# Moving transposes between TensorE and DRAM in a four-layer graph network

## The chip, the cores and the metric

The kernel runs on one core of a Trainium2 chip. The metric is device time in microseconds from launch to end, the median of several runs. The profile is of one further execution; its span goes from the first to the last instruction. All data are 32-bit floats.

## The reference

There are 64 graphs of 256 nodes with 256 features each, `x`, and a weighted adjacency, `adj`. Four graph layers follow one another; around each of them stands a residual sum and a layer norm, `x = layernorm(x + layer(x, adj))`.

```python
# layer 0: 4 heads of 64, sigmoid attention, normalised by degree
X, q, k = heads(lrelu(x @ W_lin + b_lin)), heads(lrelu(x @ W_q)), heads(lrelu(x @ W_k))
adj_h = adj[:, None] * sigmoid(einsum('bhxd,bhyd->bhxy', q, k) * scale)
dis = deg ** -0.5                       # deg: sum of adj_h over its last axis
Y = einsum('bhxy,bhyd->bhxd', dis[..., :, None] * adj_h * dis[..., None, :], X)
# then a layer norm of its own
# layer 1: 8 heads of 32, masked softmax attention
q, k, v = heads(x @ Wq + bq), heads(x @ Wk + bk), heads(x @ Wv + bv)
scores = where(adj > 0, q k^T / sqrt(32), NEG)
out = softmax(scores) v, heads joined, @ Wo + bo
# layer 2: (adj @ x + eps * x) @ W1 (256 to 1024), rms norm, silu, @ W2 (1024 to 256)
# layer 3: one head; e depends on a row term and a column term
Wh = x @ W;  e = leaky_relu(Wh.a1 [:, None] + Wh.a2 [None, :], 0.2)
h = softmax(where(adj > 0, e, NEG)) @ Wh
out = gelu(layernorm(h))
```

## The kernel before

**Tiles.** One graph is the unit of work: `graph(...)` (line 238) is called for `b` from 0 to 63 and lists the operations of all four layers. A 256x256 matrix lies in SBUF as 128 partitions by 512 words, its two row halves side by side; `two(v)` (line 166) gives it as 128 x 2 x 256.

**A planner sets the order.** No operation is issued where it is listed. `op(engine, cost, fn, writes, reads, turn=...)` records it, and `Plan.order` (line 94) then lays out all graphs at once: it keeps a clock for each engine, takes at each step the operation that can start first (ties by due time, graph and index), and gives each tile a slot in a pool when its first operation is taken. `SLOTS` (line 33) is the number of slots: 42 of 512 words (`s`), 10 of 1024 (`d`), 8 PSUM banks (`p`), 8 DRAM buffers (`h`). The order on each engine is therefore fixed before the program runs, and each engine works through its own list in order; waits between engines are by semaphore. SP issues all DMAs, through one queue, also in order.

**Turns.** ACT needs another table for Sigmoid, Exp, Silu and Gelu. Operations with these functions, and the products that feed them, carry a turn, `4 * min(b + ROUND[layer], graphs - 1 + TAIL[layer]) + function` (line 250), and a turn is worked off before the next begins. `ROUND = 0, 2, 5, 7` says how many rounds after its first layer a graph does each later one; so in the middle of the run four groups of graphs are at work in four layers in the same round. `TAIL = 0, 2, 3, 5` caps the round for the last graphs, which then share their turns.

**Transposes.** Attention weights are made with rows in the partitions, and the product that follows wants them the other way. There are two ways. `transposed` (line 266, with `transpose`, line 258) does four 128x128 transposes on TensorE into a PSUM bank; `copy` (line 297) has ACT bring that to SBUF. `far_transposed` (line 271) does 32x32 blocks with one DVE instruction into `eb` (line 275), and then lets DMAs put the blocks in place by way of a DRAM buffer `far`. With `in_order` (lines 278 to 288) these are four writes of 64 KB in pieces of 512 bytes (line 281) and four reads of 64 KB in pieces of 128 bytes (line 285). Without it, one write of 256 KB (line 289) and four reads of 64 KB (line 291), and the columns come out in another order, which the reader's pattern undoes.

Where they are used before the change:

- layer 0's output, `yb = far_transposed(ps, "yT", in_order=False)` (line 478), read by two DVE multiplications by `dis` (line 482);
- layer 1's input `xT` by TensorE (line 492); layer 1's exponentials by a far path of their own, for two heads at a time: a DVE transpose of 128x1024 (line 521), one 512 KB write (line 523) and four 128 KB reads (line 525); the product with `v1` is line 536;
- layer 3's input, `xT3 = far_transposed(x, "xT3")` (line 628), read by the product with `w3` (line 637);
- layer 3's exponentials by TensorE and ACT, `eT = copy(transposed(e), "eT")` (line 656), read by `token_major` (line 319).

**Around them.** `softmax` (line 390) masks, scales and takes the minimum on DVE (line 395) and exponentiates with a sum on ACT (line 400). Layer 1's queries get their bias from one DVE addition of 128x512 out of PSUM (line 496); the scores (line 510) need it. Layer 2 has the largest products, line 579 (to 1024 features; ACT brings them in with a bias, line 584) and line 622 (back to 256). After the layer-3 product come statistics (line 333), a power on GpSimd (line 346), an affine step (lines 383 and 386), Gelu (line 661), the residual (line 662), a last norm and the store (line 664).

Of the kernel before, what the change touches and what calls it, by code (L numbers as in the profile page):

```python
# [10 lines left out]
AF = mybir.ActivationFunctionType  # L11
OP = mybir.AluOpType

P = 128
# [5 lines left out]
PE_MM, PE_TR = 432, 109  # L20
# [6 lines left out]

WORDS = {"s": 516, "d": 1024, "b": 2048, "c": 32, "p": 512, "h": 1024}
AHEAD = 14

ROUND = 0, 2, 5, 7
TAIL = 0, 2, 3, 5
SLOTS = {"s": 42, "d": 10, "b": 3, "c": 72, "p": 8, "h": 8}


# [39 lines left out]
class Plan:  # L75
# [9 lines left out]
    def op(self, engine, cost, fn, w=(), r=(), turn=None, mode="full", after=None, size=0):  # L85
        pair = lambda x: x if isinstance(x, tuple) else (x, None)
        w, r = [pair(x) for x in w], [pair(x) for x in r]
        op = Op(engine, cost, fn, w, r, self.graph, turn, mode, after, size)
        op.table = turn is not None and engine == "ACT"
        if op.table:  # L90
            self.turns[turn] = self.turns.get(turn, 0) + 1
        self.ops.append(op)
# [73 lines left out]
def two(v):  # L166

    return v.t.rearrange("p (n c) -> p n c", n=2)
# [69 lines left out]
def graph(plan, nc, c, t, out, b):  # L238

    op = plan.op  # L240
    pe, dve, act, pool = nc and nc.tensor, nc and nc.vector, nc and nc.scalar, nc and nc.gpsimd
    NB = DB = 2
    N = D = 256
# [5 lines left out]
    def turn(layer, func):  # L249
        return 4 * min(b + ROUND[layer], plan.graphs - 1 + TAIL[layer]) + func  # L250

# [6 lines left out]
    def transpose(dst, src, w, r):  # L258

        def fn():  # L260
            for j in range(2):
                for i in range(2):
                    pe.transpose(dst()[:, j, i * P:(i + 1) * P], src()[:, i, j * P:(j + 1) * P], c.ident)  # L263
        op("PE", 4 * PE_TR, fn, [w], [r], mode="transpose")

    def transposed(src):
        ps = Value("p", "ps", 2)
        transpose(lambda: two(ps), lambda: two(src), ps, src)
        return ps

    def far_transposed(src, name, in_order=True):


        eb, far, dst = Value("s", "eb"), Value("h", "far", 4), Value("s", name, 4)
        op("DVE", 635, lambda: dve.transpose(
            eb.t.rearrange("p (b g i) -> p g b i", b=4, i=32),
            src.t.rearrange("p (n k w) -> p k n w", n=2, k=2)), [eb], [src])
        if in_order:
            F = lambda a: far.t[:64].rearrange("(a z) (y w) -> a (z y) w", a=4, w=P)[a]
            for a in range(4):  # L280
                op("SP", 420, lambda a=a: nc.sync.dma_start(
                    F(a).rearrange("(b j) w -> j b w", b=4),
                    eb.t[32 * a:32 * a + 32].rearrange("j (b w) -> j b w", b=4)), [(far, a)], [eb], after=3000, size=64)
            for a in range(4):
                op("SP", 420, lambda a=a: nc.sync.dma_start(
                    dst.t.rearrange("q (g a i) -> a q g i", g=4, a=4)[a],
                    F(a).rearrange("q (g i) -> q g i", g=4)), [(dst, a)], [(far, a)], after=4500, size=200)
            return dst
        op("SP", 420, lambda: nc.sync.dma_start(far.t[:, :512], eb.t), [(far, i) for i in range(4)], [eb], after=3000, size=256)
        for q in range(4):  # L290
            op("SP", 420, lambda q=q: nc.sync.dma_start(
                dst.t[32 * q:32 * q + 32].rearrange("j (a g) -> j a g", a=4),
                far.t[:, :512].rearrange("(a j) (b g) -> b j a g", a=4, b=4)[q]), [(dst, q)],
                [(far, i) for i in range(4)], after=4200, size=64)
        return dst

    def copy(ps, name):
        dst = Value("s", name, 2)
        op("ACT", 466, lambda: act.copy(dst.t, ps.t), [dst], [ps])  # L299
        return dst  # L300
# [109 lines left out]
    xT, adjT, x, adj = load("x0T", "xT"), load("adjT", "adjT"), load("x", "x"), load("adj", "adj")  # L410
    qk = []
    for w, name in ((c.w0_q, "qT0"), (c.w0_k, "kT0")):
        ps = feature_major(w, xT)
        y = Value("s", name)
# [3 lines left out]
    ps = token_major(xT, lambda: c.w0_l.t, [c.w0_l])  # L418
    v = Value("s", "v0")
# [20 lines left out]
    ps = Value("p", "ps")  # L440
# [18 lines left out]
    dp, dis = Value("c", "dp"), Value("c", "dis")  # L459
# [5 lines left out]
    by_head = lambda ap: ap.rearrange("p (g d) -> p g d", d=HD0)  # L465
    dis_b = lambda: dis.t[:, :8, None].to_broadcast([P, NB * H0, HD0])
    op("DVE", 603, lambda: dve.tensor_tensor(by_head(v.t), by_head(v.t), dis_b(), OP.mult), [v], [v, dis])
    ps = Value("p", "ps", 2)
# [6 lines left out]
                    pe.matmul(two(ps)[i * HD0:(i + 1) * HD0, hp, :], two(v)[:, m, h * HD0:(h + 1) * HD0],  # L475
                              A(h)[:, m, :], start=(m == 0), stop=(m == NB - 1))
    op("PE", 4 * PE_MM, fn, [ps], [v, att], mode="columns")
    yb = far_transposed(ps, "yT", in_order=False)
    y = Value("s", "y", 2)
    for i in range(2):  # L480
        by = lambda ap, i=i: ap.rearrange("p g (i k w) -> p g i k w", i=2, k=2)[:, :, i]
        op("DVE", 345, lambda y=y, i=i, by=by: dve.tensor_tensor(
            by(y.t.rearrange("p (g d) -> p g d", g=4)), yb.t.rearrange("p (i k g w) -> p i g k w", i=2, k=2, g=4)[:, i],
            dis.t[:, :8].rearrange("p (g i) -> p i g", i=2)[:, i, :, None, None].to_broadcast([P, 4, 2, 32]), OP.mult),
            [y], [yb, dis])
    mv, m = stats(y)
    affine(y, mv, m, c.g0, lambda n, xb=xb: two(xb)[:, n, :], [xb])
    x = normed(y, "x1")
# [3 lines left out]
    xT = copy(transposed(x), "xT")  # L492
    xb = plus_row(x, c.c1)
    ps = feature_major(c.w1_q, xT)
    qT1 = Value("s", "qT1")
    op("DVE", 602, lambda ps=ps: dve.tensor_tensor(two(qT1), two(ps), c.b1_q.t[:, :, None].to_broadcast([P, 2, N]), OP.add),
       [qT1], [ps, c.b1_q])

    kT1 = copy(feature_major(c.w1_k, xT), "kT1")
    v1 = copy(token_major(xT, lambda: c.w1_v.t, [c.w1_v]), "v1")  # L500
    av, r = Value("p", "av", 2), Value("c", "r")
    eTs = []
    for hq in range(H1 // 4):
        pss = [Value("p", "ps", 2) for _ in range(4)]

        def fn(hq=hq, pss=pss):
            for n in range(NB):
                for i in range(4):
                    s = slice(i * HD1, (i + 1) * HD1)
                    pe.matmul(two(pss[i])[:, n, :], two(qT1)[s, hq, n * P:(n + 1) * P], two(kT1)[s, hq, :],  # L510
                              start=True, stop=True)
        op("PE", 2 * PE_MM, fn, pss, [qT1, kT1], turn=turn(1, EXP), mode="rows")
        for pair in range(2):


            e, eb, far, eT = Value("d", "e", 4), Value("d", "eb"), Value("h", "far"), Value("d", "eT", 4)
            for i in range(2):
                softmax(pss[2 * pair + i], negmask, HD1 ** -0.5, e,
                        lambda n, i=i, e=e: e.t[:, 256 * (2 * i + n):256 * (2 * i + n + 1)],
                        lambda n, i=i: 2 * i + n, r, lambda n, h=4 * hq + 2 * pair + i: 2 * h + n, turn(1, EXP))  # L520
            op("DVE", 1155, lambda e=e, eb=eb: dve.transpose(eb.t.rearrange("p (b g i) -> p g b i", b=4, i=32),  # L521
                                                             e.t.rearrange("p (g b i) -> p g b i", b=4, i=32)), [eb], [e])
            op("SP", 420, lambda eb=eb, far=far: nc.sync.dma_start(far.t, eb.t), [far], [eb], after=3500, size=512)
            for q in range(4):
                op("SP", 420, lambda far=far, eT=eT, q=q: nc.sync.dma_start(
                    eT.t[32 * q:32 * q + 32].rearrange("j (a g) -> j a g", a=4),
                    far.t.rearrange("(a j) (b g) -> b j a g", a=4, b=4)[q]), [(eT, q)], [far], after=4000, size=128)
            eTs.append(eT)


    def fn():
        for hq in range(H1 // 4):
            for m in range(NB):
                for i in range(4):
                    h = 4 * hq + i
                    pe.matmul(two(av)[i * HD1:(i + 1) * HD1, hq, :], two(v1)[:, m, h * HD1:(h + 1) * HD1],  # L536
                              eTs[h // 2].t.rearrange("p (a h n k i) -> p h k n a i", a=4, h=2, n=2, k=2)[:, i % 2, m],
                              start=(m == 0), stop=(m == NB - 1))
    op("PE", 4 * PE_MM, fn, [av], [v1, *eTs], mode="columns")

    op("DVE", 180, lambda: dve.reciprocal(r.t[:, :16], r.t[:, :16]), [r], [r])
    ps = Value("p", "ps")
    op("PE", PE_TR, lambda ps=ps: pe.transpose(ps.t[:16, :P], r.t[:, :16], c.ident), [ps], [r], mode="transpose")
    rT, far, rb = Value("s", "rT"), Value("h", "far"), Value("s", "rb", H1)
# [7 lines left out]
    yT = Value("s", "yT")  # L552
# [72 lines left out]
    x = normed(plus(ps, xb), "x3")  # L625


    xT3 = far_transposed(x, "xT3")
    v3 = Value("s", "v3", 2)
    V3 = lambda: v3.full.rearrange("p (n c) -> p n c", n=2)  # L630
    s1 = lambda n: V3()[:, n, D:D + 1]
# [21 lines left out]
    r3 = Value("c", "r3")  # L653
    softmax(e, negmask, 1.0, e, lambda n: two(e)[:, n, :], lambda n: n, r3, lambda n: n, turn(3, EXP))
    op("DVE", 70, lambda: dve.reciprocal(r3.t[:, :NB], r3.t[:, :NB]), [r3], [r3])
    eT = copy(transposed(e), "eT")
    ps = token_major(eT, lambda: V3()[:, :, :D], [v3])
    y3 = Value("s", "y", 2)
    mv, m = stats(ps, r3)
# [91 lines left out]
```

## Time and profile before

| | |
|---|---|
| median of 3 runs | 2822.43 us (2820.94 to 2826.75) |
| the profiled execution, its own time | 2825.22 us |
| its span | 2823.4 us |
| instructions | 55149 |
| granted TensorE clock, mean | 0.991 |
| DMA queue of the kernel | 558320 packets, 475.87 MB, 59.2% of 16 engines' span |
| load of an ACT table | 1.283 us, 254 times |

In the profile PE is a TensorE matmul or transpose and PEld the load of its stationary operand, DVE is VectorE, ACT ScalarE, POOL GpSimd, and SPq the queue of DMA issues. A group of instructions is named by its line in the kernel, what it writes and reads, and its shapes; then follow its count, the time in which it was busy (overlaps counted once) and the mean duration of one. Then comes the idle time of the engine just before such instructions, with what ended it. In the chain of work that ended last, each piece begins when what released it was done, so that its pieces don't overlap and add up to the span. A DMA's time to landing is from its issue to its completion.

### The profile page before, as it was taken

How to read it: one execution, taken by the hardware profiler on the slowest of the kernel's cores; microseconds unless marked ns; L12 is line 12 of the kernel's file. 1: busy time of each engine (PE TensorE's matmuls, PEld its weight loads, DVE VectorE, ACT ScalarE, POOL GpSimd, SP SyncE). 2: the span in 40 equal slices, each digit the busy share in tenths (PEclk: the TensorE clock that was granted, in tenths of full speed). 3: DMA queues.
4: the chain of work that ended last, by engine and by line, in shares of the span. 5: the costliest groups of instructions: out<-in, count | busy, mean ns of one | idle time of the engine just before them, and what ended most of it. 6: DMA issues, size and time to landing. Idle time of an engine off the chain costs nothing.

```text
span 2823.4 us, 55149 instructions
## 1 busy us (share of the span) xinstructions
PE 2752.3 (97%) x17092; PEld 2189.6 (78%) x17092; DVE 2494.3 (88%) x7757; ACT 2131.5 (75%) x5054; POOL 585.8 (21%) x902
## 2 busy tenths in 40 slices
PE   8899999999999999999999999999999999999996
PEld 6667777887787878788878878778787778777784
DVE  5788898989899998998899989899989989899975
ACT  3767787778688777877777777878768877686774
POOL 1011211212222222212212212222212221212111
PEclk9999999999999999999999999999999999999998
DMA  4857476646466646665576556556556647475641
GB/s 142 252 151 196 152 202 180 187 134 192 127 193 199 197 135 200 192 179 148 155 192 180 172 163 183 171 167 187 174 149 183 198 141 201 125 194 153 181 123 41
DMA packets 558613, 479.40 MB, mean 170 GB/s; under 512 B 184304, under 2 KB 516976, under 8 KB 558320
## 3 DMA queue, kind: packets, MB, share of 16 engines
q1 hardware_dynamic: 558320, 475.87, 59.2%
q8 instruction: 137, 2.24, 0.4%
q14 instruction: 156, 1.28, 0.2%
HBM read 290.60 MB, written 185.07 MB: 168 GB/s over the span
## 4 chain that ended last, share of the span: by engine, by line
PE 87%; DVE 5%; ACT 3%; DMA 2%; SPq 1%; issue 1%; POOL 0%; DVEq 0%; POOLq 0%; ACTq 0%
PE ps L622 15%; PE ps L308 15%; PE ps L319 14%; PE ps L579 14%; PE ps L510 4%; PE ps L432 4%; PE ps L567 4%; PE ps L637 4%; PE ps L475 3%; PE av L536 3%; PE ps L263 2%; ACT e L400 1%; PE ps L449 1%; DVE e L395 1%; DVE st L333 1%
## 5 line engine op out<-in xcount | busy, mean ns | idle before, releaser
L400 ACT ACTIVATE e<-e,low 128x256 f32<-128x256 f32 x1152 | 575.7, 501 | 73.5 <-DVE low L395 69.8
L622 PE MATMUL ps<-w,hT 128*128 128x256 f32 x2048 | 480.6, 382 | 4.2 <-ACT hT L613 4.2
L579 PE MATMUL ps<-aggT,w 128*128 128x256 f32 x2048 | 470.8, 382 | 2.8 <-ACT aggT L299 1.4
L345 POOL TENSOR_SCALAR mv<-mv 128x2 f32<-128x2 f32 x384 | 123.0, 320 | 1624.8 <-DVE mv L335 1074.0
L579 PEld LDWEIGHTS ps<-aggT,w 128*128 128x128 f32 x2048 | 382.4, 190 | 69.2 <-issue 8.6
L622 PEld LDWEIGHTS ps<-w,hT 128*128 128x128 f32 x2048 | 381.3, 190 | 67.6 <-issue 10.5
L395 DVE CUSTOM_DVE_ANT_0 e<-ps,adj 128x256 f32<-128x256 f32 x1024 | 361.7, 420 | 33.5 <-PE ps L510 32.5
L521 DVE STREAM_TRANSPOSE eb<-e 128x1024 f32<-128x1024 f32 x256 | 310.5, 1225 | 4.7 <-ACT e L400 4.0
L346 POOL TENSOR_TENSOR mv<-mv,mhalf 128x2 f32<-128x2 f32 x384 | 307.7, 801 | 32.0
L584 ACT ACTIVATE hT<-ps,b 128x256 f32<-128x256 f32 x512 | 225.8, 473 | 97.0 <-PE ps L579 66.6
L360 ACT ACTIVATE x<-y,mv 128x256 f32<-128x256 f32 x384 | 216.2, 599 | 61.3 <-DVE mv L356 53.2
L333 DVE BATCH_NORM_STATS2 st<-y 128x6 f32<-128x256 f32 x640 | 242.3, 412 | 1.4
L400 ACT ACTIVATION_READ_ACCUMULATOR e<-e,low 128x1 f32 x1152 | 220.8, 192 | 0.0
L609 DVE SCALAR_TENSOR_TENSOR hT<-hT,r,pr 128x256 f32<-128x256 f32 x512 | 207.3, 474 | 7.0 <-PE pr L606 6.6
L590 DVE TENSOR_TENSOR sq<-sq 128x512 f32<-128x512 f32 x192 | 130.5, 680 | 48.1 <-ACT sq L587 47.0
L438 DVE TENSOR_TENSOR att<-att,adjT 128x512 f32<-128x512 f32 x256 | 165.7, 678 | 5.6 <-ACT att L436 5.5
L587 ACT ACTIVATE sq<-hT 128x512 f32<-128x512 f32 x256 | 163.1, 637 | 2.0 <-DMA far<-eb 0.6
L510 PE MATMUL ps<-kT,qT 32*128 32x256 f32 x2048 | 152.0, 404 | 1.0 <-ACT kT L299 1.0
L462 POOL TENSOR_TENSOR dp<-dp,mhalf 128x8 f32<-128x8 f32 x64 | 109.2, 1707 | 202.7 <-DVE dp L461 175.4
L436 ACT ACTIVATE att<-ps 128x512 f32<-128x512 f32 x256 | 132.3, 603 | 25.0 <-PE ps L622 18.6
L613 ACT ACTIVATE hT<-hT 128x1024 f32<-128x1024 f32 x128 | 129.8, 1051 | 19.5 <-DVE hT L609 17.0
L308 PE MATMUL ps<-x0T,w_q 128*128 128x256 f32 x512 | 132.1, 392 | 7.2 <-DMA x0T<-in_xT 7.2
(108 smaller groups left out, 5526.7 us busy)
## 6 DMA issues: line engine op xcount, KB each, us to landing
far<-eb SPq DMA_DIRECT2D x256, 512.0 KB, 3.5
eT<-far SPq DMA_DIRECT2D x1024, 128.0 KB, 3.9
adj<-in_adj SPq DMA_DIRECT2D x128, 256.0 KB, 4.7
x0T<-in_xT SPq DMA_DIRECT2D x64, 256.0 KB, 3.5
adjT<-in_adjT SPq DMA_DIRECT2D x64, 256.0 KB, 4.4
x<-in_x SPq DMA_DIRECT2D x64, 256.0 KB, 4.8
adj<-in_adjT SPq DMA_DIRECT2D x64, 256.0 KB, 5.3
far<-eb SPq DMA_DIRECT2D x64, 256.0 KB, 2.7
```

Source lines behind the costliest of these rows:

```text
L308: pe.matmul(two(ps)[:, o, :], w.t[:, k, o * P:(o + 1) * P], two(xT)[:, k, :], start=(k == 0), stop=(k == DB - 1))
L319: pe.matmul(two(ps)[:, n, :], two(xT)[:, k, n * P:(n + 1) * P], w()[:, k, :], start=(k == 0), stop=(k == DB - 1))
L333: op("DVE", 328, lambda n=n: dve.bn_stats(st.t[:, 6 * n:6 * n + 6], two(src)[:, n, :]), [(st, n)], [(src, n)])
L346: pool.tensor_tensor(m()[:, :, 2], m()[:, :, 2], c.mhalf[:, :NB], OP.pow)
L360: op("ACT", 492, lambda n=n: act.activation(two(dst)[:, n, :], two(src)[:, n, :], AF.Identity, bias=m()[:, n, 0:1], scale=m()[:, n, 2:3]), ...
L395: op("DVE", 345, lambda n=n: dve.tensor_tensor_reduce(out=E(n), in0=two(logits)[:, n, :], in1=two(negmask)[:, n, :], scale=-scale, scalar= ...
L400: op("ACT", 491, lambda n=n: act.activation(E(n), E(n), AF.Exp, bias=low.t[:, n:n + 1], scale=-1.0, accum_out=r.t[:, col(n):col(n) + 1]), ...
L510: pe.matmul(two(pss[i])[:, n, :], two(qT1)[s, hq, n * P:(n + 1) * P], two(kT1)[s, hq, :], start=True, stop=True)
L521: op("DVE", 1155, lambda e=e, eb=eb: dve.transpose(eb.t.rearrange("p (b g i) -> p g b i", b=4, i=32), e.t.rearrange("p (g b i) -> p g b i" ...
L579: pe.matmul(two(ps)[:, i, :], c.w2_1.t[:, k, (j + i) * P:(j + i + 1) * P], two(aggT)[:, k, :], start=(k == 0), stop=(k == DB - 1))
L584: op("ACT", 357, lambda ps=ps, i=i, j=j: act.activation(Hb(j + i)[:, 0], two(ps)[:, i, :], AF.Identity, bias=c.b2_1.t[:, j + i:j + i + 1]) ...
L622: pe.matmul(two(ps)[:, n, :], Hb(j)[:, 0, n * P:(n + 1) * P], c.w2_2.t[:, j, :], start=(j == 0), stop=(j == HB - 1))
```

## The change

Three numbers `NEAR = 1, 1, 3` say for how many graphs another way is taken than for the rest.

- Layer 0's output: graph 0 is transposed by TensorE and copied by ACT, and one DVE multiplication instead of two follows. All other graphs keep the DRAM way.
- Layer 1's exponentials: graph 0 by TensorE, 8 transposes and two ACT copies for each pair of heads. All others keep the DRAM way.
- Layer 3's input: graphs 61, 62 and 63 by TensorE and an ACT copy, the others through DRAM as before.
- Layer 3's exponentials: graphs 0 to 60 through DRAM, by `far_transposed` with its default `in_order`; graphs 61 to 63 by TensorE and ACT as before.
- Layer 1's query bias, all graphs: two ACT activations of 128x256 out of PSUM with the bias, one for each half, instead of one DVE addition.
- `TAIL` goes from 0, 2, 3, 5 to 0, 2, 3, 4: the last graphs' layer 3 is capped one round earlier.

```diff
+NEAR = 1, 1, 3
-TAIL = 0, 2, 3, 5
+TAIL = 0, 2, 3, 4
...
-    yb = far_transposed(ps, "yT", in_order=False)
     y = Value("s", "y", 2)
-    for i in range(2):
...
+    if b < NEAR[0]:
+        ps = transposed(copy(ps, "yT"))
+        op("DVE", 602, lambda ps=ps, y=y: dve.tensor_tensor(by_head(y.t), by_head(ps.t), dis_b(), OP.mult), [y], [ps, dis])
+    else:
+        yb = far_transposed(ps, "yT", in_order=False)
+        for i in range(2):
...
-    qT1 = Value("s", "qT1")
-    op("DVE", 602, lambda ps=ps: dve.tensor_tensor(two(qT1), two(ps), c.b1_q.t[:, :, None].to_broadcast([P, 2, N]), OP.add),
-       [qT1], [ps, c.b1_q])
+    qT1 = Value("s", "qT1", 2)
+    for o in range(2):
+        op("ACT", 357, lambda ps=ps, o=o: act.activation(
+            two(qT1)[:, o, :], two(ps)[:, o, :], AF.Identity, bias=c.b1_q.t[:, o:o + 1]), [(qT1, o)], [(ps, o), c.b1_q])
...
+            if b < NEAR[1]:
+                eT = Value("d", "eT", 2)
+                for i in range(2):
+                    half = lambda v, i=i: v.t[:, 512 * i:512 * (i + 1)].rearrange("p (n c) -> p n c", n=2)
+                    ps = Value("p", "ps", 2)
+                    transpose(lambda ps=ps: two(ps), lambda e=e, half=half: half(e), ps, e)
+                    op("ACT", 466, lambda ps=ps, eT=eT, half=half: act.copy(half(eT), two(ps)), [(eT, i)], [ps])
+                eTs.append((eT, lambda i, m, eT=eT: eT.t.rearrange("p (h m c) -> p h m c", h=2, m=2)[:, i, m]))
+                continue
...
-    xT3 = far_transposed(x, "xT3")
+    xT3 = copy(transposed(x), "xT3") if b >= plan.graphs - NEAR[2] else far_transposed(x, "xT3")
...
-    eT = copy(transposed(e), "eT")
+    eT = copy(transposed(e), "eT") if b >= plan.graphs - NEAR[2] else far_transposed(e, "eT3")
```

More of the change, by code (lines that the diff above doesn't have):

```diff
@@ L477, in graph @@
     op("PE", 4 * PE_MM, fn, [ps], [v, att], mode="columns")
-    yb = far_transposed(ps, "yT", in_order=False)
     y = Value("s", "y", 2)
-    for i in range(2):
[L481 to L485, printed above, removed]
+    if b < NEAR[0]:
[4 more added lines that the diff above has]
+        for i in range(2):
+            by = lambda ap, i=i: ap.rearrange("p g (i k w) -> p g i k w", i=2, k=2)[:, :, i]
+            op("DVE", 345, lambda y=y, i=i, by=by: dve.tensor_tensor(
+                by(y.t.rearrange("p (g d) -> p g d", g=4)), yb.t.rearrange("p (i k g w) -> p i g k w", i=2, k=2, g=4)[:, i],
+                dis.t[:, :8].rearrange("p (g i) -> p i g", i=2)[:, i, :, None, None].to_broadcast([P, 4, 2, 32]), OP.mult),
+                [y], [yb, dis])
     mv, m = stats(y)
@@ L513, in graph @@
         for pair in range(2):
-            e, eb, far, eT = Value("d", "e", 4), Value("d", "eb"), Value("h", "far"), Value("d", "eT", 4)
+            e = Value("d", "e", 4)
             for i in range(2):
@@ L520, in graph @@
                         lambda n, i=i: 2 * i + n, r, lambda n, h=4 * hq + 2 * pair + i: 2 * h + n, turn(1, EXP))
+            if b < NEAR[1]:
[7 more added lines that the diff above has]
+                continue
+            eb, far, eT = Value("d", "eb"), Value("h", "far"), Value("d", "eT", 4)
             op("DVE", 1155, lambda e=e, eb=eb: dve.transpose(eb.t.rearrange("p (b g i) -> p g b i", b=4, i=32),
@@ L527, in graph @@
                     far.t.rearrange("(a j) (b g) -> b j a g", a=4, b=4)[q]), [(eT, q)], [far], after=4000, size=128)
-            eTs.append(eT)
+            eTs.append((eT, lambda i, m, eT=eT: eT.t.rearrange("p (a h n k i) -> p h k n a i", a=4, h=2, n=2, k=2)[:, i, m]))
     def fn():
@@ L536, in fn @@
                     pe.matmul(two(av)[i * HD1:(i + 1) * HD1, hq, :], two(v1)[:, m, h * HD1:(h + 1) * HD1],
-                              eTs[h // 2].t.rearrange("p (a h n k i) -> p h k n a i", a=4, h=2, n=2, k=2)[:, i % 2, m],
+                              eTs[h // 2][1](i % 2, m),
                               start=(m == 0), stop=(m == NB - 1))
-    op("PE", 4 * PE_MM, fn, [av], [v1, *eTs], mode="columns")
+    op("PE", 4 * PE_MM, fn, [av], [v1, *(eT for eT, _ in eTs)], mode="columns")
     op("DVE", 180, lambda: dve.reciprocal(r.t[:, :16], r.t[:, :16]), [r], [r])
```

## The prediction

> **What bounds the kernel now.** I read the busy line first, then the engines by stage.
>
> ```profile
> PE 2752.3 (97%) x17092; PEld 2189.6 (78%) x17092; DVE 2494.3 (88%) x7757; ACT 2131.5 (75%) x5054; POOL 585.8 (21%) x902
> ```
>
> By stage, the columns are the stretch, its length, and then PE, PEld, DVE, ACT and POOL busy with their instructions, the clock, the DMA share and GB/s:
>
> ```profile
> 70.00:140.00 70.00, 60.71 (x359) 43.53 (x359) 56.88 (x165) 51.51 (x144) 5.25 (x6) 0.90 0.86 253
> ...
> 400.00:800.00 400.00, 398.69 (x2520) 318.67 (x2517) 358.05 (x1127) 310.67 (x743) 79.41 (x125) 1.00 0.60 168
> 800.00:1200.00 400.00, 398.07 (x2524) 317.50 (x2524) 373.89 (x1165) 317.45 (x750) 92.91 (x140) 1.00 0.64 183
> ...
> 2750.00:2824.00 74.00, 45.49 (x190) 36.44 (x188) 38.60 (x129) 33.62 (x68) 13.24 (x25) 0.82 0.17 40
> ```
>
> There are three regimes. In the middle TensorE is idle 1.3 to 1.9 us in 400, so time there is TensorE work, with DVE next at up to 93%. Between 400 and 2500 us all waits of PE that the profile lists come to 5.0 us; the longest group is this (total, times, longest):
>
> ```profile
> PE ps L308 <- ACT xT L299: 1.2, 2, 0.8
> ```
>
> At the start PE idles (400 minus its busy time, stage by stage) 29 us, 7.2 of them before the first load lands; at the end 28.5 us of the last 74. Those two stages are chains of latency, not throughput.
>
> Then the groups of instructions that the edits touch:
>
> ```profile
> L263 PE MATMUL ps<-ident,e 128*128 128x128 f32 x256 | 39.7, 277 | 2.3 <-ACT e L400 2.3
> ...
> L275 DVE STREAM_TRANSPOSE eb<-x 128x512 f32<-128x512 f32 x64 | 44.8, 701 | 5.8 <-ACT x L360 5.8
> ...
> L496 DVE TENSOR_TENSOR qT<-ps,b_q 128x512 f32<-128x512 f32 x64 | 43.5, 679 | 19.0 <-PE ps L308 18.4
> ...
> L584 ACT ACTIVATE hT<-ps,b 128x256 f32<-128x256 f32 x512 | 225.8, 473 | 97.0 <-PE ps L579 66.6 <-PE ps L622 29.9
> ...
> L299 ACT COPY eT<-ps 128x512 f32<-128x512 f32 x64 | 37.5, 586 | 26.6 <-PE ps L263 24.3 <-DMA out<-o 1.9 <-ACT v L299 0.2
> ```
>
> A transpose is said to last 277 ns and its group to be busy 39.7 us (155 ns each), but neighbours overlap. What it takes from the stream is read in the chain that ended last, whose pieces do not overlap:
>
> ```profile
> 1250.30 3.65 PE ps L579 x16
> 1253.95 0.44 PE ps L263 x4
> 1254.38 0.11 PE ps L543
> ```
>
> Four transposes hold the stream 0.44 us, 0.11 each; the same view has 0.87 for eight.
>
> **What the Trainium skill says.** (1) "Perfetto Trace Analysis", Identifying the Most-Contended Engine: matmul busy share is a poor measure, since pipelined PE instructions overlap. This trace agrees: 70.9 us by the mean (256 x 277 ns), 39.7 by the union, 28.2 (64 x 0.44) by the chain. I price with the last. (2) "VectorE: DVE Perf Modes", The three transpose paths: TensorE transposes a full 128x128 into PSUM, the DVE only 32x32 blocks, into SBUF. So the new path needs DMAs to put the blocks in place; the kernel before does just that for the layer-3 input. (3) "DMA: Bandwidth & Descriptors", Anatomy of one DMA: about 2 us of a DMA are fixed, mostly the completion. The same-sized transfers here land 1.8 and 2.6 us after issue, in agreement:
>
> ```profile
> far<-eb SPq DMA_DIRECT2D x256, 64.0 KB, 1.8
> xT<-far SPq DMA_DIRECT2D x256, 64.0 KB, 2.6
> ```
>
> (4) "ScalarE: Activation LUTs", What ACT_TABLE_LOAD costs: 1283 ns and a drain of 1380. The trace shows 1283; in the last stretch the next activation follows with no such drain, so I use 1.28 us.
>
> **The change, part by part.** Sums stand against the profiled execution: 2825.22 us, span 2823.4, so 1.8 us outside; it is 2.8 above the median 2822.43, and I take 2.8 off at the end.
>
> *Layer 3's transposes of e, 61 graphs (0 to 60).* Removed: 61 x 4 TensorE transposes, 61 x 0.44 = 26.8 us from a stream that is full: on the path. ACT loses 61 copies of 586 ns (35.7 us, off the path); one of eight PSUM banks is held less. Added: 61 DVE block transposes of 701 ns (42.8 us) and 61 x 8 DMAs on SP. Bytes are 61 x 0.52 MB = 32 MB, 6.7% of the queue's 475.9; packets are 512 of 512 B and 2048 of 128 B a graph, 156,000, 28% of the queue's 558,320. So its 59.2% share grows by 4 points (by bytes) to 17 (by packets); the 128-B ones are the cheap kind per packet, so I take 7, to about 66%, which leaves room. SP gets 4 issues of 432 and 4 of 621 ns (medians of the same two lines), 4.2 us a graph. The longer way from e to its product (0.70, then issue and 1.8, then issue and 2.6: some 8 to 10 us against 1.6 now) is covered: in the built order the two exponentials of layer 3 stand among the first three of nearly every turn on ACT, ahead of the 16 of layer 1, so between them and the Gelu that needs the result lie some 16 x (501+192) ns = 11 us plus the Silu pair. With that cover gone ACT, PE and DVE would stall behind a late Gelu.
>
> *Queries' bias.* DVE loses 64 x 679 ns = 43.5 us, ACT gains 128 x 473 = 60.5 (L584 is the same operation and shape). Net with the part above and with what graphs 0 and 61 to 63 drop (about 8 us): DVE -9 us, ACT near +30 of 2131. Neither bounds. In front of the scores the wait now stands in ACT's queue; queued behind it there are L584 and the exponentials, but ACT has 25% free and each half starts when its half of the product is ready. Zero; if ACT were late, up to 0.3 us a graph.
>
> *Graph 0 by TensorE in layers 0 and 1.* 4 + 32 transposes, +4.0 us of PE at 0.11. What they save is a trip. In the chain, graph 0's yT leaves the DVE at 37.70 and its use starts at 48.89: 11 us against about 2 by PE and an ACT copy. For the last pair of its layer-1 exponentials the chain shows
>
> ```profile
> 83.70 4.95 DMA far<-eb
> 88.67 5.00 DMA eT<-far
> ```
>
> and the product L536 starts at 104.0; the PE way ends near 82. It also takes 4.2 MB out of 70 to 140 us, where DMA is 86% busy. Of PE's 22 us idle in the first 400 (beyond the first load) I take 7 back; bounds 0 (graph 1 still goes through DRAM and sets the ramp) and 14.
>
> *Last three graphs' layer-3 input by TensorE; last turn one earlier.* Before, in the timeline of the last graph:
>
> ```profile
> 2784.91 1.09 ACT L360 ACTIVATE x<-y,mv 128x256 f32<-128x256 f32 x2 [3.15 <-DVE mv L356]
> ...
> 2786.03 0.71 DVE L275 STREAM_TRANSPOSE eb<-x 128x512 f32<-128x512 f32 x1 [0.61 <-ACT x L360]
> ...
> 2788.64 2.54 SPq L285 DMA_DIRECT2D xT<-far  x4
> ...
> 2796.55 3.65 PE L637 MATMUL ps<-w,xT 128*128 128x258 f32 x8
> ```
>
> From x to its product 10.5 us; by PE 0.44 and a copy of 0.59, with hand-overs 1.2: -9.3. The built order has two table loads fewer (252 for 254); one on the path: -1.3. Against that, four graphs instead of three now share the last Gelu turn: after the last product, before, 15.5 us remain (2807.88 to 2823.4); the new DVE order has 15.3 us of work there, by my count at the page's durations, plus a pow and the store: +2.5. Sum -8; bounds -14 and -2 (graphs 62 and 63 in each other's way). The 12 extra transposes (1.3 us) fall where PE idles.
>
> *Order of the rest.* The planner reorders everything. Counted in the two built orders, PE changes between full, row, column and transpose shapes 1049 times before and 1051 after: no gain or loss. New waits in the middle: 0 to 8 us (PE now waits 0.10 us a graph); I take 2.5.
>
> Sum: -26.8 + 4.0 - 7 - 8 + 2.5 = -35.3; 2825.2 - 35.3 = 2789.9, less 2.8: **2787**.
>
> **Rivals.** *The waits come back* (0.08). DVE, at 93% in places, or the later eT3, makes PE wait 0.4 us a graph: 61 x 0.4 = 24 us, and the ends give little (-4 in all, with the +4.0 paid): 2822 - 27 + 24 - 0 = 2819. For: DVE is close behind. Against: its work per graph is unchanged and PE's 5.0 us of waits show that the order absorbs it.
>
> *SP's queue, slower* (0.05). SP issues in order; eight DMAs a graph, half of them waiting for the other half to land (1.8 us), stand before layer 1's transfers. Up to 4.2 + 1.8 = 6 us of delay meet L536, whose slack the trace does not show. It turns slower when PE loses over (35.3+5.6)/61 = 0.67 us a graph; at 1.0 it is 2787 + 61 = 2848. Against: no PE wait on eT<-far stands in the list for the middle, and SP is issuing about half the time.
>
> *Both ends shrink fully* (0.07): -26.8 + 4 - 18 - 14 = -55: 2768.
>
> *The change doesn't do what it says:* the built PE order has 196 transposes fewer (244 out, 48 in), so that is excluded.
>
> **Chances.** Forecast 0.80. Its own range: -26.8+4-14-14 = -51 to -26.8+4-0-2+8 = -17, so 2771 to 2806. A measurement here can tell about 0.2%, 5.6 us, from no change. Faster: 0.80 + 0.07 + half of the first rival = 0.91; same 0.04; slower 0.05. The range 2771 to 2806 leaves out some 2 in 10.
>
> **What would show it.** PE instructions 16896, group L263's e at 12, PE's busy time 20 to 24 us less. In the middle PE idle still under 3 us in 400; if more, the wait list names DVE (first rival) or DMA eT (second). DMA share near 66%. L536's first start near 80 instead of 104. The last 74 us with some 8 less idle. I am wrong if PE's waits in the middle pass 15 us or the last stretch is no shorter.

## The result, and the profile after

The changed kernel takes 2799.0 us (four runs, 2796.7 to 2804.5) against 2822.1 us before, a ratio of 0.9918 with a 95% interval of 0.9899 to 0.9937: 23 us less. The forecast was 2787, with a range of 2771 to 2806. The profiled execution after is the fastest of its four, 2796.7 us with a span of 2794.9 us; the one before was 2825.22 and 2823.4. The spans differ by 28.5 us.

Engines first, from the page of the changed kernel:

```profile
PE 2728.7 (98%) x16896; PEld 2159.8 (77%) x16896; DVE 2477.0 (89%) x7745; ACT 2150.8 (77%) x5131; POOL 590.6 (21%) x902
```

TensorE has 196 instructions and 23.6 us of busy time less, as expected, DVE 17 us less, ACT 19 more. By stage (columns as before: stretch, length, then PE, PEld, DVE, ACT, POOL, the clock, the DMA share, GB/s):

```profile
70.00:140.00 70.00, 65.41 (x423) 49.23 (x423) 57.78 (x169) 52.16 (x136) 8.85 (x11) 0.92 0.61 183
...
400.00:800.00 400.00, 399.56 (x2496) 317.07 (x2495) 371.41 (x1170) 323.60 (x777) 91.66 (x137) 1.00 0.70 191
800.00:1200.00 400.00, 396.29 (x2476) 313.47 (x2474) 360.09 (x1125) 312.56 (x745) 79.73 (x126) 1.00 0.66 184
...
2000.00:2400.00 400.00, 390.00 (x2407) 307.69 (x2407) 355.32 (x1118) 308.91 (x756) 84.41 (x125) 0.99 0.66 180
...
2720.00:2795.00 75.00, 54.30 (x263) 45.12 (x260) 48.38 (x162) 37.33 (x77) 15.66 (x30) 0.91 0.13 33
```

The start and the end are shorter: PE idles 4.6 us instead of 9.3 between 70 and 140, where the DMA share fell from 0.86 to 0.61, and 20.7 us of the last 75 instead of 28.5 of the last 74. The middle is worse: between 400 and 2400 us PE was never idle for 2 us in a stretch of 400, and now it is for 3.7 and for 10.0. PE's waits between 400 and 2500 us, longest first (total, times, longest):

```profile
PE ps L516 <- ACT kT L300: 6.9, 3, 5.9
PE ps L653 <- DVE hT L625: 2.9, 2, 2.7
PE ps L638 <- ACT hT L600: 1.5, 2, 1.2
PE ps L613 <- DVE sq L608: 1.5, 1, 1.5
```

The queue's share rose to about what was forecast (66%). The small pieces are indeed cheap one by one: over the trace before, a packet of 128 bytes took 13.5 ns of a DMA engine on average, one of 1 KB 59.3 ns.

```profile
q1 hardware_dynamic: 710624, 501.59, 65.1%
```

At the end, the last graph's layer-3 input now takes this way in the timeline:

```profile
2765.32 0.60 ACT L361 ACTIVATE x<-y,mv 128x256 f32<-128x256 f32 x1
...
2768.37 2.01 PE L653 MATMUL ps<-w,xT 128*128 128x258 f32 x8 [0.97 <-ACT xT L300]
```

From the start of x to its product it is 3.05 us instead of 11.64.

The difference of the two spans, put together from PE's busy and idle time (idle is the length of a stretch less PE's busy time in it):

| | forecast | measured | before to after |
|---|---|---|---|
| PE busy (-26.8 + 4.0 + 1.3) | -21.5 | -23.6 | 2752.3 to 2728.7 |
| idle in the first 400 us | -7 | -12.5 | 29.1 to 16.6 |
| idle, 400 to 2600 us | +2.5 | +12.8 | 10.7 to 23.5 |
| idle, 2600 us to the end | -9.3 | -5.2 | 31.4 to 26.2 |
| sum | -35.3 | -28.5 | of 28.5 |

(-9.3 is the forecast's -8 with its 1.3 us of transposes hidden in idle time.) The term that failed is the third: the new waits in the middle.

### The profile page after: what moved, and what is told of

It is laid out like the page before. It is cut to its first block, busy times and chain, and to the rows that moved or that the text cites. A ratio compares the mean times of both kernels' runs of the same rounds, so it can differ in the third digit from the quotient of the medians.

```text
span 2794.9 us, 55587 instructions
## 1 busy us (share of the span) xinstructions
PE 2728.7 (98%) x16896; PEld 2159.8 (77%) x16896; DVE 2477.0 (89%) x7745; ACT 2150.8 (77%) x5131; POOL 590.6 (21%) x902
## 4 chain that ended last, share of the span: by engine, by line
PE 81%; DVE 7%; ACT 5%; DMA 3%; SPq 2%; issue 1%; POOL 0%; DVEq 0%; POOLq 0%; ACTq 0%
PE ps L309 15%; PE ps L320 14%; PE ps L638 13%; PE ps L595 13%; PE ps L516 4%; PE ps L433 4%; PE ps L476 4%; PE av L552 4%; PE ps L583 4%; PE ps L653 3%; ACT e L401 2%; DMA eT<-far 1%; PE ps L450 1%; PE ps L264 1%; DVE st L334 1%
## 5 line engine op out<-in xcount | busy, mean ns | idle before, releaser
L595 PE MATMUL ps<-aggT,w 128*128 128x256 f32 x2048 | 476.7, 384 | 5.3 <-DVE low L396 3.1
L346 POOL TENSOR_SCALAR mv<-mv 128x2 f32<-128x2 f32 x384 | 129.8, 338 | 1610.2 <-DVE mv L336 1056.1
L625 DVE SCALAR_TENSOR_TENSOR hT<-hT,r,pr 128x256 f32<-128x256 f32 x512 | 207.2, 473 | 17.8 <-PE pr L622 17.8
L437 ACT ACTIVATE att<-ps 128x512 f32<-128x512 f32 x256 | 132.2, 602 | 27.8 <-PE ps L638 25.1
```

What stands on the lines that cost most here:

```text
L595: pe.matmul(two(ps)[:, i, :], c.w2_1.t[:, k, (j + i) * P:(j + i + 1) * P], two(aggT)[:, k, :], start=(k == 0), stop=(k == DB - 1))
```

## The experiments

Each of the twelve other kernels is measured beside the kernel before on the same chip; since three chips were used, kernels of different experiments are best compared by their ratios (0.001 is 2.8 us). The table has PE's busy time and idle time by stage from each profile; "far" is the DRAM way of layer 3's exponentials, "bias" the queries' bias on ACT, "ends" the rest of the change. A profile is one execution, up to 6 us from its kernel's median, so differences of 2 or 3 us in these columns say little.

| kernel | what it is | median us | ratio, 95% interval | PE busy | idle, first 400 | 400 to 2600 | last 75 (ends rounded to 1 us) | clock |
|---|---|---|---|---|---|---|---|---|
| before | | 2822.1 to 2825.5 | 1 | 2752.3 | 29.1 | 10.7 | 27.5 | 0.991 |
| order_before | another order | 2820.2 | 0.9980 (0.9972-0.9988) | 2749.5 | 29.0 | 9.6 | 28.4 | 0.992 |
| bias_only | bias | 2821.8 | 0.9986 (0.9980-0.9993) | 2749.9 | 27.1 | 12.4 | 27.7 | 0.992 |
| ends_only | ends | 2803.7 | 0.9927 (0.9915-0.9940) | 2744.8 | 19.4 | 11.0 | 17.8 | 0.995 |
| no_far | ends, bias | 2802.7 | 0.9930 (0.9917-0.9942) | 2752.1 | 13.5 | 13.2 | 18.0 | 0.995 |
| far_only | far | 2821.4 | 0.9988 (0.9980-0.9996) | 2736.5 | 33.9 | 18.9 | 27.8 | 0.989 |
| no_bias | ends, far | 2820.0 | 0.9977 (0.9969-0.9986) | 2735.5 | 22.6 | 26.8 | 20.7 | 0.991 |
| after | ends, bias, far | 2799.0 | 0.9918 (0.9899-0.9937) | 2728.7 | 16.6 | 23.5 | 20.7 | 0.993 |
| order_a | after, another order | 2811.5 | 0.9946 (0.9933-0.9958) | 2731.0 | 17.0 | 31.0 | 19.4 | 0.989 |
| order_b | after, a third order | 2803.1 | 0.9920 (0.9906-0.9934) | 2732.1 | 16.9 | 21.0 | 20.4 | 0.992 |
| store_pool | after, stores off SP | 2797.8 | 0.9901 (0.9887-0.9914) | 2725.9 | 17.6 | 21.4 | 23.6 | 0.995 |
| light_far | after, light trip | 2787.6 | 0.9871 (0.9856-0.9886) | 2726.6 | 15.8 | 17.1 | 20.5 | 0.994 |
| hidden4 | after, 4 large buffers | 2802.2 | 0.9926 (0.9912-0.9939) | 2734.8 | 14.5 | 26.5 | 19.6 | 0.992 |
| hidden4_no_far | the same without far | 2825.9 | 1.0004 (0.9994-1.0014) | 2758.4 | 17.6 | 27.8 | 16.6 | 0.992 |

My theory after the result: the three gains are real, and the DRAM way gives part of its gain back through waits in the middle, by way of the DMAs it adds to SP's queue. The rivals: the bias on ACT makes the waits; the new order is just less lucky.

### far_only

```diff
# on the kernel before
-    eT = copy(transposed(e), "eT")
+    eT = copy(transposed(e), "eT") if b >= plan.graphs - 3 else far_transposed(e, "eT3")
```

> Only one part of the change, made alone on the kernel before: layer 3's exponentials of graphs 0 to 60 through DRAM. My theory: TensorE loses 61 x 0.44 = 26.8 us of work, and the extra DMAs on SP's queue and the work beside it give some 10 us of waits back, so about 2822 - 27 + 10 = 2805, with PE idle of 15 to 20 us between 400 and 2400 us (5.4 before). If the waits come from the queries' bias on ACT instead: PE idle there stays near 5 us and the time is about 2796. If the waits come only from the luck of a new order: anything from 2795 to 2810.

It gained 3.7 us, not 17. PE's busy time fell 15.8 us, but idle time rose by 4.8 in the first 400 us and by 8.2 from 400 to 2600. The rest is at the end: from 2600 us on there are 4.4 us more, with one wait of 7.3 us of layer 3's product for its transposed exponentials from DRAM (`eT<-far`), at 2786.8 of 2825 us. The changed kernel has no such wait. The idle time between 400 and 2400 us, 18.9 us, is what my theory said, and it came without the bias, so the bias is not needed to make it; the time was worse than every expectation.

### bias_only

```diff
# on the kernel before
-    qT1 = Value("s", "qT1")
-    op("DVE", 602, ...)
+    qT1 = Value("s", "qT1", 2)
+    for o in range(2):
+        op("ACT", 357, ...)
```

> Only the queries' bias on ACT, made alone on the kernel before. My theory: it moves 43.5 us from DVE and puts 60.5 us on ACT and no engine is bound there, so 2822 give or take 5. If the bias on ACT is what makes PE wait: PE idle between 400 and 2400 us rises from 5.4 to about 15 and the time to about 2832.

2821.8 against 2825.1: about nothing, as forecast. DVE fell 41.5 us and ACT rose 59.3.

### ends_only

```diff
# on the changed kernel
-    eT = copy(transposed(e), "eT") if b >= plan.graphs - NEAR[2] else far_transposed(e, "eT3")
+    eT = copy(transposed(e), "eT")
# and the bias on DVE as before
```

> Only the two ends, made on the kernel before: graph 0 by TensorE in layers 0 and 1, the layer-3 input of the last three graphs by TensorE, the last turn one earlier; exponentials of layer 3 by TensorE for all graphs and the bias on DVE as before. My theory: the start gives 12 us less PE idle in the first 400 us and the end 6 to 8, less 4 us of added transposes: about 2822 - 15 = 2807. If the ends give nothing (graph 1 and the last norm set them): 2822 to 2826.

2803.7: 21 us gained, more than the whole forecast for the ends (-7 + 4 - 8 = -11) and nearly all that the full change gives. The start has 9.7 us less idle time, the last 75 us 9.7 less (6.1 less from 2600 us on). PE's busy time fell 7.5 us too, although 48 transposes were added. The mean clock granted is 0.995 instead of 0.991, but that is not shown to be the cause: no_far, below, has the same PE instructions and the same mean clock, and 2752.1 us. Graph 0, the last three graphs and `TAIL` were not measured one by one.

### no_bias

The changed kernel with the diff of bias_only undone.

> The changed kernel without the queries' bias on ACT: that is one DVE addition again. My theory: the bias part is worth nothing by itself, but without it DVE has 43.5 us more, 2520 us of 2795 or 90%, so the same or up to 5 us slower: 2799 to 2804. If the bias on ACT is what makes PE wait in the middle: about 2789, with PE idle between 400 and 2400 us near 6.

2820.0: 21 us slower than the changed kernel, 17 by the ratios, and outside both expectations. DVE is at 2517.5 us, 89% of the span. But one order stands here against one order, and the next two runs show how far orders of the same work lie apart. No_bias is slower than all three of them, than the slowest by 9 us (by the ratios); the idle time of the middle, 26.8 us, is inside what they have (21.0 to 31.0).

### order_a, order_b, order_before

```diff
-    op("DVE", 180, lambda: dve.reciprocal(r.t[:, :16], r.t[:, :16]), [r], [r])
+    op("DVE", 190, lambda: dve.reciprocal(r.t[:, :16], r.t[:, :16]), [r], [r])
# order_b: 170; order_before: 190 on the kernel before
```

> The changed kernel, with one number of the planner changed that has no meaning for the work (the cost that it assumes for one reciprocal, 190 for 180): the same instructions, another order on every engine. If the order's luck decides some us: the time differs from 2799 by 3 to 10 us either way, and the waits of PE in the middle are other ones. If the waits are a property of the change itself (more transfers, DVE nearer to its limit): PE idle between 400 and 2400 us is again 15 to 25 us and the time within 3 us of 2799.

> As the last one, with the assumed cost 170 for 180: a third order of the same instructions. The same two expectations: by luck, a time 3 to 10 us from 2799 and other waits; as a property of the change, PE idle of 15 to 25 us between 400 and 2400 us and a time within 3 us of 2799.

> The kernel before, with the assumed cost of that reciprocal 190 for 180: its instructions in another order. If the 5.4 us of PE idle between 400 and 2400 us in the kernel before were a lucky order: 10 to 20 us here and 2826 to 2837. If they are what this work leaves: 3 to 8 us again and 2819 to 2826.

The same instructions in three orders took 2799.0, 2803.1 and 2811.5 us, a spread of 12.5 (8 by the ratios). In order_a 21 us of idle time lie between 2400 and 2600 us; its longest group of waits from 400 to 2600, and the stretch:

```profile
PE ps L583 <- ACT x L361: 18.8, 6, 8.2
...
2400.00:2600.00 200.00, 179.03 (x1069) 138.48 (x1068) 166.43 (x516) 142.33 (x331) 41.31 (x61) 0.94 0.62 162
```

So both expectations hold in part: the times differ by luck, yet from 400 to 2600 us no order of the changed kernel came near the 10 us of the two orders of the kernel before (order_before: 2820.2 us, the second expectation in time). Of the kernels with three large buffers, the five without the DRAM way have 9.6 to 13.2 us of idle time between 400 and 2600 us (mean 11.4), the five with it and its full trips, on SP for the stores too, 18.9 to 31.0 (mean 24.2). The stretch matters. From 400 to 2400 us, which these expectations named, order_a has only 10.0 us and order_before 9.4; the five without the DRAM way have 5.4 to 12.5 (mean 9.7) and the five with it 10.0 to 22.9 (mean 17.4), so there order_a lies inside the other group.

### no_far

The line of ends_only, with the bias kept.

> The changed kernel with layer 3's exponentials by TensorE for all graphs; the ends and the bias stay. The ends alone gave 2804, and the DRAM way without the bias gave next to nothing, twice. If the DRAM way is worth its 26.8 us once DVE is relieved by the bias: about 2799 + 20 = 2819. If it is worth little in any company: 2797 to 2806, with PE idle between 400 and 2600 us near 11 instead of 23.5.

2802.7: the second expectation. In this company too the DRAM way is worth about 4 us, which the overlapping intervals don't tell from nothing, and against order_a and order_b nothing. PE's busy time is 23.4 us higher than after, its idle time from 400 to 2600 us 10.3 lower.

### store_pool

```diff
-    op("SP", 420, lambda: nc.sync.dma_start(out[b]...
+    op("SP", 420, lambda: nc.gpsimd.dma_start(out[b]...
```

> The changed kernel with its 64 output stores issued by GpSimd's queue instead of SP's; the order on TensorE, DVE and ACT is left exactly as it is. In the changed kernel one store stood behind eight transfers on SP, its buffer came free late, ACT idled 6.0 us for it and PE 5.9 us. If SP's queue behind its transfers is what gives time back: that wait is gone, PE idle between 400 and 2400 us falls from 19.8 to 14 or less, and the time falls by 5 to 8 us to about 2792. If the waits are those of DVE and ACT alone: unchanged within 2 us, about 2799.

The wait that it aims at is this one, in the timeline of the changed kernel (start, length, then what; in brackets the idle time before and what ended it):

```profile
2330.82 0.74 DVE L365 TENSOR_SCALAR o<-y,mv 128x256 f32<-128x256 f32 x2 [0.61 <-POOL mv L347]
...
2332.78 5.81 SPq L541 DMA_DIRECT2D eT<-far  x8
...
2338.80 0.39 SPq L680 DMA_DIRECT2D out<-o  x1
...
2342.85 0.63 ACT L603 ACTIVATE sq<-hT 128x512 f32<-128x512 f32 x1 [6.00 <-DMA out<-o]
2343.38 0.57 ACT L300 COPY kT<-ps 128x512 f32<-128x512 f32 x1
...
2344.00 2.09 PE L516 MATMUL ps<-kT,qT 32*128 32x256 f32 x16 [5.92 <-ACT kT L300]
```

A store stood behind eight reads in SP's queue: its data were ready at 2331.56, and it was issued 7.2 us later. Its buffer is the next one for `sq` on ACT, so ACT stood still for 6.0 us, and with it kT's copy and PE. With the stores on GpSimd's queue, PE waits 1.28 us at this place, and its waits between 400 and 2600 us begin with

```profile
PE ps L516 <- ACT kT L300: 3.4, 3, 1.8
```

That long wait is gone, but other small ones grew: idle time from 400 to 2600 us is 21.4 instead of 23.5, the time 1.2 us lower and inside the interval of the changed kernel. It is the second expectation. The late store is a true stall, but taking it away by itself gains almost nothing. (GpSimd pays for the issues with 47 us more of busy time; whether that made other waits grow is not shown.)

### light_far

```diff
# in far_transposed, used with light=True for graphs 0 to 60 of layer 3's exponentials
             for a in range(4):
-                op("SP", 420, lambda a=a: nc.sync.dma_start(
+                op("SP", 420, lambda a=a: (a == 0 and nc.sync.dma_start(far.t[:, :512], eb.t)) if light else nc.sync.dma_start(
...
             for a in range(4):
-                op("SP", 420, lambda a=a: nc.sync.dma_start(
+                op("SP", 420, lambda a=a: (a == 3 and nc.sync.dma_start(dst.t, far.t[:, :512])) if light else nc.sync.dma_start(
```

> The changed kernel with the DRAM trip of layer 3's exponentials made light: one contiguous write and one contiguous read of 256 KB instead of four and four in small pieces, 2 issues on SP for 8, 256 packets for 2560 a graph; the blocks do not get to their places, so layer 3's product uses the blocks in another arrangement. The order on PE, DVE and ACT is left as it is. If transfers and SP's queue make the new waits: PE idle between 400 and 2600 us falls from 23.5 to about 11 and the time to about 2787. If the waits lie in the order that the planner writes down, or on DVE: idle stays at 18 to 24 and the time at 2794 to 2799.

This kernel leaves out the placing of the 32x32 blocks, so it doesn't compute layer 3; it only shows what the trips cost.

2787.6, the first expectation in time: 11.4 us less than the changed kernel, 13 by the ratios. The bytes are the same (501.57 MB), the packets 146,400 fewer, and the queue's share

```profile
q1 hardware_dynamic: 564224, 501.57, 62.5%
```

fell by 2.6 points. At the place shown above the store still stands behind eight reads of layer 1, but SP has got further: the store is issued 3.2 us after its data are ready instead of 7.2, and PE's wait is 1.83 us instead of 5.92:

```profile
2325.22 5.60 SPq L541 DMA_DIRECT2D eT<-far  x8
...
2327.00 0.74 DVE L365 TENSOR_SCALAR o<-y,mv 128x256 f32<-128x256 f32 x2 [0.61 <-POOL mv L347]
...
2330.91 0.40 SPq L680 DMA_DIRECT2D out<-o  x1
...
2335.97 1.15 PE L516 MATMUL ps<-kT,qT 32*128 32x256 f32 x16 [1.83 <-ACT kT L300]
```

The instructions of PE, ACT and DVE stand in the same order as in the changed kernel (as they do in store_pool), so this comparison is free of the luck of orders. Idle time between 400 and 2600 us is 17.1 us, between the two expectations and 6.4 less: half of the 12.9 by which the groups with and without the DRAM way differ. (From 400 to 2400 us it is 6.2 less, of 7.7.) So the trip's six further DMAs and small pieces make about half of the new waits or more. 4.1 of the 6.4 us are the one wait shown. SP's issues, added up over each trace, take 1505 us in the kernel before, 1762 in the changed kernel and 1526 with the light trip; whether it is SP's time, the small pieces or the length of the trip that counts is not separated. What stays with a light trip lies in the order, in DVE's added transposes, in the two DMAs left, or simply in a PE that has less work and so overtakes the others more often; these runs do not separate those.

### hidden4, hidden4_no_far

```diff
-SLOTS = {"s": 42, "d": 10, "b": 3, "c": 72, "p": 8, "h": 8}
+SLOTS = {"s": 40, "d": 10, "b": 4, "c": 72, "p": 8, "h": 8}
# hidden4_no_far: also the line of ends_only
```

> The changed kernel with four instead of three buffers for layer 2's hidden rows and layer 0's attention, paid with 40 instead of 42 of the 512-word buffers. In the changed kernel PE's waits in the middle are scattered ones for ACT and DVE; if layers 0 and 2 of neighbouring graphs wait for these three large buffers, PE idle between 400 and 2600 us falls to about 10 and the time to 2780 to 2788, faster than both kernels. If buffers are not what is short: 2797 to 2805.

> The last kernel with layer 3's exponentials by TensorE for all graphs: a second pair for what the DRAM way is worth. If the 26.8 us of TensorE's work come through when buffers are there: some 15 to 20 us slower than hidden4. If the DRAM way is worth little: within 8 us of it.

The fourth buffer gained nothing: 2802.2. Without the DRAM way the same kernel takes 2825.9, so here that way is worth 24 us, 22 by the ratios and more than either expectation, all of it PE's busy time (2758.4 to 2734.8). Both have nearly the same idle time in the middle (26.5 and 27.8 us); one stretch of it is

```profile
1600.00:2000.00 400.00, 390.81 (x2408) 308.43 (x2408) 358.25 (x1114) 307.76 (x729) 86.43 (x133) 1.00 0.62 182
```

for hidden4 and

```profile
1600.00:2000.00 400.00, 392.93 (x2463) 312.52 (x2462) 351.60 (x1119) 314.97 (x750) 83.32 (x126) 0.99 0.56 169
```

for hidden4_no_far. This goes against my theory that the waits come with the DRAM way alone: an order can have them without it.

## Why the prediction was right, and where it was not

**The sum held, in part by luck.** The forecast gave 24.3 of its 35.3 us to the DRAM way (26.8 less 2.5 of new waits) and 11 to the ends. Measured alone, the ends give 21 of the 23 us and the DRAM way some 4. The total stayed in the range because the start was worth more than forecast while the waits in the middle ate up most of the DRAM way. Of the 12 us between forecast and median, 6.8 are in the profiled execution (2789.9 against 2796.7); 5.1 are the step from it to the median, which I took as -2.8 and was +2.3.

**"On the path: 61 x 0.44 = 26.8 us."** The direction was right: PE's busy time falls in all four pairs. The size was roughly so in the two pairs with the bias, 23.4 and 23.6 us, and not in the two without it, 15.8 and 9.3. Why is not shown. The mean clock is lower by 0.002 and 0.004 in the latter, but that does not settle it: ends_only and no_far, with the same PE instructions and a clock of 0.995, are 7.3 us apart, and store_pool (0.995) and order_a (0.989), again with the same PE instructions, only 5.1. What failed is the claim that it stays a gain: by the ratios, four pairs give -3 (far_only), +14 (no_bias), -3 (against no_far) and -22 us (hidden4) for the DRAM way, a mean of -4, where the forecast had 26.8 less 2.5 of waits.

**"New waits in the middle: I take 2.5; bounds 0 and 8."** The mis-sized term: 12.8 us, past the upper bound and past the 15 us at which the prediction said it would be wrong there (idle time from 400 to 2400 us is 19.8). I read 5.0 us of waits as room; they held for the DMA queue and the order as they were, and my list ended at 2500 us (to 2600 PE's idle time before is 10.7 us, with one wait of 4.3 us). light_far puts about half of the difference or more on the trips. That is the mechanism of the second rival (SP in order, given a chance of 0.05) at a small part of its price, and not at its place: in the changed kernel's list for the middle the product L552 does not wait for its data. At the one place traced, a buffer behind a late transfer comes free late, and ACT waits for it.

**"Covered": the longer way from e to its product.** This held: in the middle no wait of PE for layer 3's late exponentials is listed for the changed kernel. The sum behind it was off, though. The 192 ns that I added for each exponential overlap the next one (in the trace before they start about 0.51 us apart at 1280 us), so 16 take 8.2 us and not 11; but much other work stands there too, and from those exponentials to the next Gelu it is 30 us. In far_only, where one such trip fell at the very end, PE waited 7.3 us for it.

**A long wait costs more than its length.** The Trainium skill, "TensorE: Matmul & The Clock Gate", Why this matters for your kernels, says that TensorE idle for more than about 3 us falls back to half its clock. The trace agrees: in order_a, after PE waits of 7.98 and 8.21 us, eight matmuls took 3.91 us each time instead of 1.89,

```profile
2532.22 3.91 PE L583 MATMUL ps<-adj,x 128*128 128x256 f32 x8 [7.98 <-ACT x L361]
```

and in the changed kernel sixteen took 2.09 instead of 1.15 after 5.92 us, with a granted clock of 0.50 from 2344 to 2347 us; after light_far's 1.83 us the same sixteen took 1.15. The prediction priced a wait at its length only. That is small here, 0.9 us for the one long wait of the changed kernel and 2.0 us for each of the two in order_a.

**"Graph 0 by TensorE: 7 back."** Right in kind, too small: 12.5 us less idle time, with L552 starting at 83.2 instead of 104.0 (forecast near 82). In the ten kernels with the ends it is 13.5 to 22.6; in the four without the ends, 27.1 to 33.9.

**"Last three graphs: -8."** The trip was priced well: 8.6 us saved from x to its product, for 9.3. From the end of the last large layer-2 block to the end of the span it is 51.2 us instead of 61.4, so -10.1; the idle time of the last 75 us is 16.6 to 23.6 in all kernels with the ends and 27.5 to 28.4 in those without. Before that stretch 2 us are lost again (3.5 to 5.6 from 2600 us on).

**"Queries' bias: zero."** By itself nearly so, twice: -3.3 us on the kernel before, within 1 us on ends_only. Together with the DRAM way it looks like 21 us (17 by the ratios) from one order of each, and like 9 against the slowest order of the changed kernel; with one order of no_bias that is not enough. What the bias is worth there stays open.

**What stays open.** What makes the rest of the middle's waits, and whether the DRAM way is worth anything once orders are averaged. Which part of the ends gives how much: graph 0, the last three graphs' input and `TAIL` were changed together in every run. Among the kernels that compute the whole, store_pool and the changed kernel are fastest and not to be told apart (0.9901 and 0.9918, intervals that overlap); ends_only, with none of the 488 added DMAs, is 4.7 us behind the latter (2.5 by the ratios, and their intervals overlap too).

## What to carry to other kernels

Work taken off a full engine is a gain only until the next thing is late: price the move's transfers as queue entries too, since in an in-order DMA queue a late transfer also returns its buffer late, to an instruction that has nothing to do with it. Where the start and the end are chains of latency, a shorter trip for the first and the last tiles alone can be worth more than a change to nearly all of them: here 21 us from four graphs of 64 and one turn less. Where a planner orders the work, measure two or three orders of the same instructions before a difference of half a per cent is given a cause.

## What was not expected of the hardware

The prediction did not reckon with matmuls at about half speed after a PE wait of 6 to 8 us, eight to sixteen of them each time. Nor did it expect how little the queue's share says: sixty-one trips in small pieces (2560 pieces of 128 and 512 bytes a trip) took only 2.6 points more of the 16 DMA engines than the same bytes in 256 pieces, yet cost 11.4 us of the kernel's time by the medians.
